# Three products of 12-bit parts for the plain own products of two layers of a graph network

## The chip, the cores and the metric

The kernel runs on one core of one Trainium2 chip. The metric is the device time of one execution in microseconds; the times shown are of three runs, and one further execution was profiled. In what follows PE is the matrix engine, PEld its weight loads, DVE the vector engine, ACT the scalar engine, POOL the general engine and SP the engine that only issues DMAs. Each engine works through its instructions in order.

## The reference

```python
def _edge_conv(x, src, dst, W, b):
    m = jnp.concatenate([x[dst], x[src] - x[dst]], axis=-1) @ W + b
    s = jax.ops.segment_sum(m, dst, num_segments=N)
    cnt = jax.ops.segment_sum(jnp.ones((dst.shape[0],), m.dtype), dst, num_segments=N)
    return s / jnp.maximum(cnt, 1.0)[:, None]

h = jnp.maximum(_layernorm(x, axis=-1), 0.0)
xs = [h]
for W, b in ((W0, b0), (W1, b1), (W2, b2)):
    h = jax.nn.relu(_edge_conv(h, src, dst, W, b))
    xs.append(h)
return x + jnp.concatenate(xs, axis=-1) @ Wf + bf
```

There are 2500 nodes of 256 features, 80000 edges sorted by destination, and three layers. With W split into its upper half Wt (for the destination) and its lower half Wb (for the difference), the sum over the edges of one destination is its degree times h(Wt - Wb), the "own" part, plus the product of a matrix of edge counts with z = h Wb.

## The kernel before

Nodes are padded to 20 tiles of 128 (NT); two tiles are a pair q, ten pairs. Features are kept turned, feature by node, in `hT` (two halves of 128 features, `hT[:, 0]` and `hT[:, 1]`), already multiplied by the degree, and `share` divides again where it is needed. The destinations are cut into five window groups, four of 504 columns and a last one, `alone`, of 486. `a_dram` holds the counts of edges, sources by destinations, one tensor to a group.

**Layer 0** builds the counts of one group while it multiplies those of the group before. `finish(g)` (line 904) stores a group's counts with four DMAs, from POOL's queue (from SP's for `alone`); for group 0 it also adds x to `acc` by accumulating DMAs (`add_x`, line 826). `acc`, 20 tiles of 256 columns in SBUF, collects the result. When group 4 begins, SP stores it to `acc_dram` (line 1136); layers 1 and 2 add their share there with accumulating DMAs on POOL's queue, and the bias bf is added there by four more (`add_bf`, line 1109), in layer 1's stream. In layer 0 the own products of groups 1 to 4 are already made of 12-bit parts: `split_own` (line 1083) makes three parts of hT (ACT rounds a high part, DVE subtracts to a low one, DVE combines both to a third), `forms_of_own` three of the weights, and three products in the fast float format replace one plain one.

**Layers 1 and 2** have two phases each. In the **node phase** (the loop over Q + LAG iterations, line 1431 on) each iteration multiplies one pair of node tiles by Wb and Wf with 12-bit parts (`Nodes.multiply`, from a `Split` of hT and `Forms` of the weights), ACT and DVE scale the result and split it into `zh` and `zl`, a high and a low part, sums for the later scheme go to `sh` and `sl`, and the pair of two iterations earlier (LAG = 2) is multiplied by the counts of `alone` (`Alone.multiply`). The lone group's own products are four plain ones, `own` (line 1350): two in early iterations, two in `end`. In the **stream phase** (`Stream.run`, line 1404) the other four groups go in two pairs by a scheme of seven products for a two by two block product. Chunk c of a pair (c = 0 to 4) has seven steps; a step multiplies one block by parts of z or of the sums, two tiles by a high and a low part each, so four products of 504 columns. That makes 70 steps, numbered 0 to 69, the second pair's from 35. The steps of a chunk are called b11, b21, b22, r1, r2, r3, r4. `Pair.make` (line 1260) makes their blocks out of a staged chunk: ACT casts five, DVE adds for r1 and r2 in place and makes r3 and r4 alone. Blocks are made LEAD = 5 steps ahead; there are seven buffers `block`. In chunk 4 each step has one more product, the own one, plain, of `ws` or the sums `wsum` of the weights with hT or sums of hT (`own_sum`, line 1276; `Pair.multiply`, line 1291). `take` (line 1308) then combines the seven results into hT. So there are 7 x 2 x 2 = 28 own products of pairs in the two layers.

The pool `stage` has four buffers of a chunk (1.0 MB from `a_dram`, two DMAs on SP). `Stream.make` asks for chunk m + 3 when chunk m is made. The node phase and the end of the stream use the same buffers for splits of hT. What is done besides, at a step n, stands in `tick` (line 1461): the combination of the weights, bf, the splits of the next layer's first node pairs, the next layer's forms, and, in layer 2, two loads of `acc_dram` back into `acc`.

**The end** multiplies the ten pairs of node tiles by the last part of Wf; DVE scales by `share` and adds `acc` (`add_to_acc`, line 1203), and the rows are stored.

Of the kernel before, what the change touches and what calls it, by code (L numbers as in the profile page):

```python
# [313 lines left out]
def by_windows(ctx: ExitStack, tc: tile.TileContext, x, src, dst, Ws, bs, Wf, bf, out, missing):  # L314
# [67 lines left out]
    acc = const.tile([P, NT, D], F32, name="acc")  # L382
# [3 lines left out]
    zl = const.tile([P, 2, Q * D + 32], F32R, name="zl")  # L386
    key_m = early.tile([P, NW + 1, CH, REP], BF16, name="key_m")
# [7 lines left out]
    ident_b = const.tile([P, P], BF16, name="ident_b")  # L395
    iota_m = const.tile([P, P], BF16, name="iota_m")
    iota_n = const.tile([P, NB], BF16, name="iota_n")
    deg = const.tile([P, WG, W + 1], F32, name="deg")
    gsum = const.tile([P, WG, W + 5], F32, name="gsum")
    nc_ = const.tile([P, W + 2], F32, name="nc_")  # L400
    deg_b = const.tile([P, WG, W + 1], BF16, name="deg_b")
    below = const.tile([P, CH, WG], F32, name="below")
    back_b = const.tile([P, P + 1], BF16, name="back_b")
# [59 lines left out]
    def load_wf(l, queue=SP):  # L463
        if l == L:
# [439 lines left out]
    def finish(g, a):  # L904
# [6 lines left out]
        if g == 0:  # L911
            for t in range(0, NT, 5):
                add_x(t, t + 5)
        yield
# [194 lines left out]
    def add_bf(k):  # L1109

        POOLo.dma_start(acc_dram[:, 5 * k:5 * k + 5, :],
                        bass.AP(tensor=bf.tensor, offset=bf.offset, ap=[[0, P], [0, 5], [1, D]]), accum_op=OP.add)

# [7 lines left out]
    for g in range(NG):  # L1121
        at = {}
        own = [NT] * 4 if g == 0 else [3, 3, 8, 8]
        if g + 1 < NG:
# [10 lines left out]
        else:  # L1135
            SPo.dma_start(acc_dram, acc)
# [35 lines left out]

    tmps = ctx.enter_context(tc.tile_pool(name="tmps", bufs=6))
    stage = ctx.enter_context(tc.tile_pool(name="stage", bufs=4))
    late = ctx.enter_context(tc.tile_pool(name="late", bufs=1))
    sh = late.tile([P, 2, Q * D + 32], F32R, name="sh")
    sl = late.tile([P, 2, Q * D + 32], F32R, name="sl")
    wsum = late.tile([P, 4, P], F32, name="wsum")

# [22 lines left out]

    def add_to_acc(t, po):
        DVEo.scalar_tensor_tensor(acc[:, t, :], po, share[:, t:t + 1], acc[:, t, :], op0=OP.mult, op1=OP.add)
# [41 lines left out]

    class Pair:

        def __init__(self, l, i):
            self.l, self.i = l, i  # L1250
            self.one, self.two = (slice(c0, c0 + n) for c0, n in map(group_of, pairs[i]))
            self.bank, self.r = {}, {}
# [23 lines left out]
        def own_sum(self, i):  # L1276
            one, two, r = self.one, self.two, self.r
            if i == 0:
                r["r1"] = tmp()[:, :GS]
                DVEo.tensor_add(r["r1"], hT[:, 0, one], hT[:, 0, two])  # L1280
            elif i == 1:
                r["r2"] = tmp()[:, :GS]
                DVEo.tensor_add(r["r2"], r["r1"], hT[:, 1, two])
            elif i == 2:
                r["r3"] = tmp()[:, :GS]
                DVEo.tensor_sub(r["r3"], hT[:, 0, one], r["r2"])
            elif i == 3:
                r["r4"] = tmp()[:, :GS]
                DVEo.tensor_add(r["r4"], r["r2"], hT[:, 1, one])

        def multiply(self, c, part, what, made):
# [3 lines left out]
            if c == Q // 2 - 1:  # L1295
                if part[0] == "x":
                    w = ws[self.l][0][:, part[2], part[1] * P:(part[1] + 1) * P]
                else:
                    w = wsum[:, part[1], :]
                m = {"b11": hT[:, 0, self.one], "b21": hT[:, 1, self.one], "b22": hT[:, 1, self.two]}.get(what)  # L1300
                PEo.matmul(to, w, self.r[what] if m is None else m, start=False, stop=False)
            for k, j in enumerate((2 * c, 2 * c + 1)):
                for z in range(2):
                    unit[0] = PEo.matmul(to, part_of(part, z, j), made[what][:, k, :],
                                         start=(c == 0 and k == 0 and z == 0),
                                         stop=(c == Q // 2 - 1 and k == 1 and z == 1))
# [27 lines left out]
    class Alone:  # L1334
# [15 lines left out]
        def own(self, o, c):  # L1350
            PEo.matmul(self.to[o], ws[self.l][0][:, c, o * P:(o + 1) * P],
                       hT[:, c, self.c0:self.c0 + self.n], start=(c == 0), stop=(c == DC - 1))

        def end(self):
            for o in range(DC):
                self.own(o, 1)
# [5 lines left out]
    def load_first(order):  # L1362
        c = order[0] // 2
        st = stage.tile([P, 4 * GS], F32R, name="staged").rearrange("p (t n) -> p t n", n=GS)
# [202 lines left out]
```

## Time and profile before

| | us |
|---|---|
| median of three runs | 462.43 |
| lowest, highest | 462.11, 462.63 |
| the profiled execution | 462.09 |
| its span, first to last instruction | 460.2 |
| node phase of layer 1 | 192.0 to 239.3 |
| stream of layer 1 | 239.3 to 315.4 |
| node phase of layer 2 | 315.4 to 364.2 |
| stream of layer 2 | 364.2 to 440.1 |
| the end's products | 440.1 to 455.7 |

The granted clock of PE was 1.000 over the whole span. Nearly all instructions have line 282 in the trace, that of the helper which keeps them in order, so they are told apart by tile names and shapes. A plain product of floats shows as two records, a product in the fast float format as one; both have the type f32 in the trace. Products are pipelined: one of 504 columns is shown as 0.39 us long, though the next may start before it ends. A row of a timeline may merge several instructions (x6); its duration is then from the first start to the last end.

### The profile page before, as it was taken

How to read it: one execution, taken by the hardware profiler on the slowest of the kernel's cores; microseconds unless marked ns; L12 is line 12 of the kernel's file. 1: busy time of each engine (PE TensorE's matmuls, PEld its weight loads, DVE VectorE, ACT ScalarE, POOL GpSimd, SP SyncE). 2: the span in 40 equal slices, each digit the busy share in tenths (PEclk: the TensorE clock that was granted, in tenths of full speed). 3: DMA queues.
4: the chain of work that ended last, by engine and by line, in shares of the span. 5: the costliest groups of instructions: out<-in, count | busy, mean ns of one | idle time of the engine just before them, and what ended most of it. 6: DMA issues, size and time to landing. Idle time of an engine off the chain costs nothing.

```text
span 460.2 us, 7512 instructions
## 1 busy us (share of the span) xinstructions
PE 452.0 (98%) x2729; PEld 356.6 (77%) x2729; DVE 353.2 (77%) x676; ACT 308.9 (67%) x595; POOL 62.6 (14%) x95
## 2 busy tenths in 40 slices
PE   8999999999999999999999999999999999999995
PEld 4888877677778778878878868867788787688685
DVE  7999979899888946178758758886877487569795
ACT  4878878694945434377769839756776897597540
POOL 4770006101001000022151000000212000000000
PEclk9999999999999999999999999999999999999999
DMA  8320088982908249685899999626578957520014
GB/s 277 101 58 13 1 171 130 204 174 42 184 1 168 60 171 432 230 231 118 208 333 183 193 186 208 110 90 184 66 154 215 354 184 291 204 92 0 1 64 164
DMA packets 30489, 71.90 MB, mean 156 GB/s; under 512 B 2427, under 2 KB 19150, under 8 KB 29550
## 3 DMA queue, kind: packets, MB, share of 16 engines
q1 hardware_dynamic: 17886, 47.71, 31.3%
q0 software_dynamic: 10784, 21.77, 28.7%
q10 hardware_dynamic: 1776, 1.89, 1.2%
q8 instruction: 22, 0.36, 0.3%
q14 instruction: 21, 0.17, 0.1%
HBM read 45.45 MB, written 28.69 MB: 161 GB/s over the span
## 4 chain that ended last, share of the span: by engine, by line
PE 94%; DVE 2%; DMA 2%; issue 0%; SPq 0%; DVEq 0%
PE bank L282 86%; PE pz L282 8%; DMA wbf<-in_L_gnn_Wf_dram 2%; PE turned L282 1%; DVE one_n L282 1%; DVE one_m L282 1%; DVE own_h L282 0%; DVE hT L282 0%; SPq L282 0%; DVE deg L282 0%; DVE acc L282 0%; DVE away L282 0%; DVE deg_b L282 0%; DVEq L282 0%
## 5 line engine op out<-in xcount | busy, mean ns | idle before, releaser
L282 ACT CAST block<-staged 128x1008 fp32r<-128x1008 bf16 x100 | 97.2, 1031 | 17.0 <-DVE staged L282 6.0
L282 PE MATMUL bank<-a,zh 128*128 128x504 f32 (+1 forms) x200 | 82.0, 410 | 0.0
L282 PE MATMUL bank<-a,zl 128*128 128x504 f32 (+1 forms) x200 | 77.9, 389 | 0.0
L282 PE MATMUL bank<-block,zh 128*128 128x504 f32 (+1 forms) x184 | 76.9, 418 | 0.0
L282 ACT CAST a<-bank 128x480 fp32r<-128x480 f32 (+1 forms) x105 | 54.3, 561 | 31.2 <-PE bank L282 30.9
L282 DVE TENSOR_TENSOR one_m<-iota_m,key_m 128x2048 bf16<-128x2048 bf16 (+2 forms) x55 | 64.1, 1165 | 9.4 <-PE bank L282 9.1
L282 PE MATMUL bank<-block,zl 128*128 128x504 f32 (+1 forms) x184 | 71.2, 387 | 0.0
L282 PE MATMUL bank<-block,sh 128*128 128x504 f32 x160 | 68.9, 431 | 0.0
L282 PE MATMUL bank<-block,staged 128*128 128x512 f32 (+1 forms) x288 | 62.8, 369 | 0.0
L282 PE MATMUL bank<-block,sl 128*128 128x504 f32 x160 | 62.6, 391 | 0.0
L282 PEld LDWEIGHTS bank<-block,staged 128*128 128x128 f32 x288 | 49.3, 188 | 10.2 <-issue 0.9
L282 DVE TENSOR_TENSOR block<-staged 128x1008 fp32r<-128x1008 bf16 x40 | 47.0, 1205 | 5.0 <-PE bank L282 3.5
L282 ACT ACTIVATE tmp<-bank,share 128x256 f32<-128x256 f32 x78 | 34.4, 471 | 23.8 <-PE bank L282 15.9
L282 POOL DMA_DIRECT2D acc_dram<-tmp x20 | 17.1, 853 | 191.9 <-ACT tmp L282 191.9
L282 PEld LDWEIGHTS bank<-a,zh 128*128 128x128 f32 x200 | 37.7, 188 | 6.6 <-ACT a L282 0.3
L282 PEld LDWEIGHTS bank<-a,zl 128*128 128x128 f32 x200 | 37.7, 189 | 6.2 <-issue 0.2
L282 DVE TENSOR_TENSOR one_n<-iota_n,key_n 128x640 bf16<-128x640 bf16 (+2 forms) x110 | 42.5, 428 | 0.0
L282 PEld LDWEIGHTS bank<-block,zh 128*128 128x128 f32 x184 | 34.6, 188 | 9.9 <-issue 2.3
L282 PEld LDWEIGHTS bank<-block,zl 128*128 128x128 f32 x184 | 34.6, 188 | 9.8 <-issue 3.2
L282 DVE TENSOR_TENSOR staged<-staged 128x1008 bf16<-128x1008 bf16 x40 | 27.2, 679 | 18.0 <-ACT block L282 15.8
L282 PEld LDWEIGHTS <-one_m 128*128 128x128 bf16 x834 | 30.3, 98 | 13.7 <-issue 7.0
L282 PE MATMUL pz<-wbf,hT 128*128 128x256 f32 x160 | 38.5, 385 | 0.2 <-DMA wbf<-in_L_gnn_Wf_dram 0.2
(195 smaller groups left out, 676.1 us busy)
## 6 DMA issues: line engine op xcount, KB each, us to landing
staged<-a_dram SPq DMA_DIRECT2D x40, 504.0 KB
a_dram<-a POOLq DMA_DIRECT2D x16, 630.0 KB, 7.8
block<-a_dram SPq DMA_DIRECT2D x16, 504.0 KB
acc_dram<-tmp POOLq DMA_DIRECT2D x20, 256.0 KB, 4.9
a_dram<-a SPq DMA_DIRECT2D x4, 1260.0 KB
acc_dram<-acc SPq DMA_DIRECT2D x1, 2560.0 KB
acc_dram<-in_L_gnn_bf_dram POOLq DMA_DIRECT2D x4, 640.0 KB, 33.2
acc<-acc_dram SPq DMA_DIRECT2D x2, 1280.0 KB
```

The source lines that it names most:

```text
L282: return self.tc.keep_in_program_order(call(*args, **kwargs))
```

## The change

- **Own products.** 23 of the 28 own products of the pairs, and the last two of the four of the lone group in each layer, become three products of 12-bit parts. In layer 1 r3 and r4 of the second pair stay plain, in layer 2 r2, r3 and r4. Each layer's weights are split once into `pair_w` (`PairForms`, on `ws` and on `wsum`), in the node phase. The split of the moving side is made by `own_high` (one ACT instruction) and `own_rest` (two DVE instructions) into one of three places in `spare`.
- **Where they stand.** The own product moves from chunk 4 to chunk 0 (b11, b21) or 2 (b22, r1) in the first pair, and to chunk 2 (b11, b21, b22) in the second (`OWN_AT`). `PLAN` lists, for each step, which job is done; steps -9 to -3 are iterations of the node phase. It takes the place of `tick`.
- **Buffers.** `stage` has three buffers; the splits of the first node pairs of the next layer use the places in part. The lone group's first blocks are loaded into `spare` in layer 1 and into two blocks in layer 2. The chunk loads are asked for from iteration 8 on.
- **Bias and acc.** The bias is added to `acc` in SBUF by four accumulating DMAs behind the stores of group 2 in layer 0; `acc` is stored to `acc_dram` when group 3 begins. Its memory is then free. At the end its copy is loaded from `acc_dram` into `zl` and `zh` by six DMAs (`back`, step 63 of layer 2), DVE adds from there and writes to a `tmp` that is stored.

```diff
-    acc = const.tile([P, NT, D], F32, name="acc")
+    acc = early.tile([P, NT, D], F32, name="acc")
...
         if g == 0:
             for t in range(0, NT, 5):
                 add_x(t, t + 5)
+        if g == 2:
+            for t in range(0, NT, 5):
+                POOLo.dma_start(acc[:, t:t + 5, :],
+                                bass.AP(tensor=bf.tensor, offset=bf.offset, ap=[[0, P], [0, 5], [1, D]]), accum_op=OP.add)
...
+        if g + 2 == NG:
+            SPo.dma_start(acc_dram, acc)
...
-    stage = ctx.enter_context(tc.tile_pool(name="stage", bufs=4))
+    stage = ctx.enter_context(tc.tile_pool(name="stage", bufs=3))
...
+    spare = late.tile([P, 9 * 512], F32R, name="spare")
+    pair_w = late.tile([P, 3, 2, 4 * P], F32R, name="pair_w")
+    places = [[spare[:, (3 * i + k) * 512:(3 * i + k + 1) * 512] for k in range(3)] for i in range(3)]
...
+    class PairForms:
+        def high(self):
+            ACTo.activation(self.parts[0], self.raw, AF.Copy, scale=C1 * DOWN)
+        def low(self):
+            DVEo.scalar_tensor_tensor(self.rest, self.raw, C1, self.parts[0].bitcast(F32), op0=OP.mult, op1=OP.subtract)
+        def across(self):
+            ACTo.activation(self.parts[1], self.rest, AF.Copy, scale=E12)
+        def less(self):
+            DVEo.scalar_tensor_tensor(self.rest, self.parts[0].bitcast(F32), -1.0 / E12, self.rest, op0=OP.mult, op1=OP.add)
+        def last(self):
+            ACTo.activation(self.parts[2], self.rest, AF.Copy, scale=1.0 / C1)
+
+    OWN_AT = [{"b11": 0, "b21": 0, "b22": 2, "r1": 2}, {"b11": 2, "b21": 2, "b22": 2}]
...
+        def own_high(self, what, place):
+            h = self.own_of(what)
+            self.own[what] = [p[:, :GS] for p in places[place]]
+            ACTo.activation(self.own[what][0], self.r[what] if h is None else h, AF.Copy, scale=DOWN)
+
+        def own_rest(self, what):
+            h = self.own_of(what)
+            high, low, across = self.own[what]
+            DVEo.tensor_sub(low, self.r[what] if h is None else h, high.bitcast(F32))
+            DVEo.scalar_tensor_tensor(across, low.bitcast(F32), -E12, high.bitcast(F32), op0=OP.mult, op1=OP.add)
...
-            if c == Q // 2 - 1:
+            own_at = OWN_AT[self.i].get(what, last)
+            if c == own_at:
+                if what in self.own:
+                    w = (1, part[1]) if part[0] == "s" else (0, 2 * part[2] + part[1])
+                    for k, p in enumerate(self.own.pop(what)):
+                        PEo.matmul(to, pair_w[:, k, w[0], w[1] * P:(w[1] + 1) * P], p, start=(c == 0 and k == 0), stop=False)
...
         def end(self):
             for o in range(DC):
-                self.own(o, 1)
+                for k in range(3):
+                    PEo.matmul(self.to[o], pair_w[:, k, 0, (2 + o) * P:(3 + o) * P], self.parts[k], start=False, stop=(k == 2))
...
+    PLAN = [{
+        -9: "form.0.high combine", -8: "form.0.low form.1.high", -7: "form.0.across form.1.low", -6: "form.0.less form.1.across alone_high.2",
+        -5: "form.0.last form.1.less alone_rest high.0.b11.0", -4: "form.1.last rest.0.b11 high.0.b21.1", -3: "rest.0.b21",
+        5: "high.0.b22.2 sum.0.r1", 7: "rest.0.b22", 8: "high.0.r1.0", 10: "rest.0.r1", 11: "sum.0.r2",
+        13: "high.0.r2.1", 15: "rest.0.r2", 17: "sum.0.r3", 19: "high.0.r3.2", 21: "rest.0.r3", 22: "sum.0.r4", 24: "high.0.r4.0", 26: "rest.0.r4",
+        36: "high.1.b11.1", 38: "rest.1.b11", 39: "high.1.b21.0", 41: "rest.1.b21", 42: "high.1.b22.2", 44: "rest.1.b22", 45: "less",
+        46: "sum.1.r1", 48: "sum.1.r2", 50: "high.1.r1.1", 51: "sum.1.r3", 52: "rest.1.r1 sum.1.r4", 53: "high.1.r2.2 node.0.0", 54: "rest.1.r2",
+        55: "node_rest.0", 57: "node.1.-", 59: "node_rest.1", 60: "node.2.-", 62: "node_rest.2", 64: "next", 65: "next_low", 66: "next_across", 67: "next_last",
+    }]
+    PLAN.append({**PLAN[0], 45: "", 53: "node.0.0", 54: "", 63: "back", 65: "next_low node.3.-", 68: "node_rest.3", 69: "begin"})
...
+        def back():
+            for z, a, b in ((zl, 16, NT), (zh, 0, 8), (zh, 8, 16)):
+                q = a % 16 // 2
+                for i in range(2):
+                    SPo.dma_start(z[:, i, q * D:(q + (b - a) // 2) * D].bitcast(F32).rearrange("p (q d) -> p q d", d=D),
+                                  acc_dram[:, a + i:b:2, :])
...
+            if i >= Q - 2:
+                stream.load((1, 1, 2, 3)[i - Q + 2])
...
-            add_to_acc(t, po[k])
+            DVEo.scalar_tensor_tensor(sums[:, k, :], po[k], share[:, t:t + 1], acc_of(t), op0=OP.mult, op1=OP.add)
```

More of the change, by code (lines that the diff above doesn't have):

```diff
@@ L1360, in by_windows, with load_first @@
     loaded = {}
[L1362 to L1365 removed]
+    def load_first():
+        st = spare[:, :4 * GS].rearrange("p (t n) -> p t n", n=GS)
+        SPo.dma_start(st.bitcast(F32), a_dram[alone][:, 0:4, :])
         for p in range(2):
[L1367 to L1368 removed]
+            loaded[p] = st[:, 2 * p:2 * p + 2, :]
     def load_alone(p, order):
@@ L1426, in by_windows, with next_forms, jobs @@
         if l == 1:
-            load_first(order)
-            split(order[2])
+            load_first()
+            split(order[2]).rest()
         pending = []
         stream = Stream(l)
+        after = orders[l + 1]
+        two = stream.steps[0][1], stream.steps[-1][1]
+        new_raw(l + 1)
+        forms = PairForms(l, 0, ws[l][0].rearrange("p c n -> p (c n)")), PairForms(l, 1, wsum.rearrange("p s n -> p (s n)"))
+        nodes = {}
+        def next_forms():
+            raw = flat(l + 1)
+            coming[:] = [Forms(raw, [raw[:, c, :] if l + 1 < L else raws[L][:, c, 0, :] for c in range(DC)])]
+            coming[0].high()
+        def back():
[4 more added lines that the diff above has]
+                                  acc_dram[:, a + i:b:2, :])
+        jobs_of = {
+            "sum": lambda i, r: two[i].own_sum(r), "high": lambda i, w, k: two[i].own_high(w, k), "rest": lambda i, w: two[i].own_rest(w),
+            "alone_high": lone.high, "alone_rest": lone.rest,
+            "combine": lambda: combine(wsum, ws[l][0].rearrange("p c (o n) -> p (c o) n", o=2)),
+            "form": lambda i, step: getattr(forms[i], step)(),
+            "node": lambda k, place: nodes.update({k: split(after[k], place)}), "node_rest": lambda k: nodes[k].rest(),
+            "less": lambda: DVEo.tensor_sub(ws[l + 1][0], ws[l + 1][0], ws[l + 1][1]),
+            "next": next_forms, "next_low": lambda: coming[0].low(), "next_across": lambda: coming[0].across(),
+            "next_last": lambda: coming[0].last(), "begin": lambda: begun.append(split_in_blocks(6, False)), "back": back,
+        }
+        def jobs(n):
+            for job in PLAN[l + 1 == L].get(n, "").split():
+                name, *args = job.split(".")
+                jobs_of[name](*(int(a) if a.isdigit() else None if a == "-" else a for a in args))
         for i in range(Q + LAG):
@@ L1440, in by_windows @@
                 if i + AHEAD_H < Q and order[i + AHEAD_H] not in splits:
[L1441 removed]
+                    split(order[i + AHEAD_H]).rest()
                 pending.append(n)
```

132 lines of the change are left out of this document (56 added, 76 removed).

## The prediction

> **What bounds the kernel now.** I read the page's busy shares and the chain that ended last, then the busy time by stage.
>
> ```profile
> PE 452.0 (98%) x2729; PEld 356.6 (77%) x2729; DVE 353.2 (77%) x676; ACT 308.9 (67%) x595; POOL 62.6 (14%) x95
> PE 94%; DVE 2%; DMA 2%; issue 0%; SPq 0%; DVEq 0%
> 239.30:315.40 76.10, 76.10 (x310) 57.80 (x309) 57.88 (x76) 55.99 (x64) 2.70 (x2) 1.00 0.83 167
> 364.20:440.10 75.90, 75.90 (x310) 57.62 (x309) 57.02 (x77) 55.05 (x64) 0.00 (x0) 1.00 0.38 134
> ```
>
> The first line is the page's, the second the chain's; the other two are stretches (length, then busy time of PE, weight load, DVE, ACT and POOL, granted clock, DMA share, GB/s): the pair streams of layers 1 and 2, 70 steps each. PE is busy throughout at clock 1.00, and 94% of the chain is PE. A busy PE need not be at its peak, so what a product costs is read from the distance of starts. In the streams DVE is busy 57.88 of 76.10 us and ACT 55.99: these two have room, and the question is how much of it the change uses up.
>
> **The change part by part.**
>
> *The products.* The timeline of PE gives the prices.
>
> ```profile
> 245.80 0.39 PE L282 MATMUL bank<-block,zh 128*128 128x504 f32 x1
> 252.19 0.39 PE L282 MATMUL bank<-block,zh 128*128 128x504 f32 x1
> 302.94 1.00 PE L282 MATMUL bank<-hT,wt 128*128 128x504 f32 x2
> 313.50 1.01 PE L282 MATMUL bank<-tmp,wt 128*128 128x504 f32 x2
> 275.60 1.01 PE L282 MATMUL bank<-tmp,wt 128*128 128x504 f32 x2
> 237.70 1.79 PE L282 MATMUL bank<-hT,wt 128*128 128x486 f32 x4
> 239.56 0.39 PE L282 MATMUL bank<-block,zl 128*128 128x504 f32 x1
> 137.36 0.85 PE L282 MATMUL bank<-own_h,own_w 128*128 128x504 f32 x3
> 172.92 1.48 PE L282 MATMUL bank<-own_h,own_w 128*128 128x486 f32 x6
> L282 PEld LDWEIGHTS bank<-own_h,own_w 128*128 128x128 f32 x48 | 8.6, 189 | 1.3
> ```
>
> From 245.80 to 252.19 lie seven steps of four products: 6.39/28 = 0.228 us each, 0.913 a step. From 302.94 to 313.50 lie six steps that have a plain own product as well: 10.56/6 = 1.760 a step, so a plain own product (two records) costs 0.847. The three products that replace it are already in the trace, in layer 0: three of 504 columns end 0.85 after the first starts, which is two distances of 0.23 and the 0.39 of the last. Three cost 0.685, and each replacement saves 0.162 us. Twelve of the pairs' products change in layer 1 (all but r3 and r4 of the second pair) and eleven in layer 2 (r2 too stays plain): 23 x 0.162 = 3.73 us. Of the lone group's own products the two of the second half change in each layer. Today's two take 239.56 - 0.228 - 237.70 = 1.63 us, one 0.816 (a product of the stream stands between them and 239.56). Six in 1.48 us are five distances of 0.22 and one length of 0.38, so three cost 0.66: 4 x 0.156 = 0.62. **PE loses 4.35 us.** The added weight loads (three for two) stay under the products, as layer 0's 0.19 do under 0.22.
>
> The Trainium skill, FP8 and Floating Point Precision, TensorE Precision Notes, says that a true FP32 product makes four passes through the array. Four of the stream's products would be 0.913 us; the trace has 0.847, so the rule is nearly right and the rows decide; by it the change would save 27 x 0.228 = 6.2 us.
>
> *The splits.* Each takes one ACT and two DVE instructions.
>
> ```profile
> L282 ACT ACTIVATE own_h<-hT 128x504 fp32r<-128x504 f32 x6 | 3.8, 636 | 4.8 <-PE bank L282 2.2 <-DVE hT L282 2.1 <-ACT a L282 0.5
> 240.00 5.69 ACT L282 CAST block<-staged 128x1008 fp32r<-128x1008 bf16 x6
> 274.62 0.67 DVE L282 TENSOR_TENSOR hT<-bank,tmp 128x504 f32<-128x504 f32 x1
> 275.21 0.67 DVE L282 TENSOR_TENSOR staged<-staged 128x1008 bf16<-128x1008 bf16 x1
> 278.30 2.31 DVE L282 TENSOR_TENSOR block<-staged 128x1008 fp32r<-128x1008 bf16 x2
> 309.12 0.69 DVE L282 TENSOR_TENSOR staged<-hT,staged 128x512 fp32r<-128x512 f32 x1
> 309.84 0.69 DVE L282 SCALAR_TENSOR_TENSOR staged<-staged 128x512 fp32r<-128x512 f32 x1
> 244.08 0.42 DVE L282 TENSOR_TENSOR wsum<-wt 128x256 f32<-128x256 f32 x1
> 244.53 0.62 DVE L282 TENSOR_TENSOR wsum<-wsum,wt 128x128 f32<-128x128 f32 x2
> 214.50:219.00 4.50, 4.50 (x22) 3.68 (x21) 3.46 (x8) 3.27 (x8) 0.84 (x1) 1.00 0.75 177
> 228.00:232.50 4.50, 4.50 (x22) 3.70 (x21) 2.48 (x6) 2.34 (x5) 0.85 (x1) 1.00 1.06 341
> ```
>
> A split costs ACT 0.64. DVE's instructions start 0.60 apart where they are independent (274.62 and 275.21), the two large ones that make blocks 1.12 each, and one that needs the result before it comes 0.72 later (309.12 and 309.84): a split is 0.72 + 0.60 = 1.32.
>
> Layer 1's stream gets ten splits: DVE 57.88 + 13.2 - 1.0 (the combination of the weights, 0.42 and 0.62, goes into the node phase) = 70.1 us, ACT 55.99 + 6.4 = 62.4 us. PE will need 76.10 - 12 x 0.162 = 74.2. Both fit in total, DVE narrowly. The tightest place is the second pair of layer 1, from step 41 to step 62. Between the last block made for each, DVE has three chunks of blocks (each 2 x 0.60 + 2 x 1.12 = 3.44), six splits, four own sums and the difference of the next weights: 10.3 + 7.9 + 2.4 + 0.6 = 21.2 us. PE takes 21 x 0.913 + 3 x 0.685 = 21.2 us for these steps. So there DVE works as long as PE, and what keeps PE from waiting is the lead it starts with: the two blocks of 278.30 are done at 280.61, step 35 began at 277.4 (275.60 and one plain step) and step 41 begins 6 x 0.913 later, at 282.9, 2.3 us after its block is there. That lead stays unless DVE itself waits. If the cover goes, PE is late by what DVE waited beyond 2.3 us. In layer 2 one split and the difference are missing, 1.9 us more room.
>
> In the node phase an iteration is 4.5 us of PE, with DVE busy 3.46 and ACT 3.27 (2.48 and 2.34 in the last two, which split no nodes). Over seven iterations DVE gets 1.0 + 4 x 0.6 + 3 x 1.32 = 7.4 us of 5 x 1.04 + 2 x 2.02 = 9.2, ACT nine instructions of 0.64, 5.8 of 10.5. The fullest iteration (a weight step and the lone group's split) overruns by 0.9 us; the zl that is then late is read two iterations later. I take nothing for this; without that cover 0.9 us a layer.
>
> I put 0.35 us for small stalls (from nothing to 4 us), near the nothing that the balance gives.
>
> *Staging in three buffers.* A chunk's load now waits until the chunk three before it is made into blocks.
>
> ```profile
> 245.80:252.20 6.40, 6.40 (x30) 5.26 (x29) 5.01 (x6) 6.34 (x7) 0.00 (x0) 1.00 0.98 196
> 383.40:389.80 6.40, 6.40 (x30) 5.26 (x29) 3.61 (x5) 4.92 (x6) 0.00 (x0) 1.00 0.88 321
> ```
>
> From then to its first use are 14 steps less the 5 of lead, 8.2 us. A chunk is 1.0 MB: 5.3 us at the 196 GB/s of layer 1, 3.2 at the 321 of layer 2. It fits, and layer 1 also loses the bias traffic. I take nothing; if it took 9.2 us, PE would wait up to 1 us in each of seven chunks.
>
> *The bias and acc.* Four accumulating DMAs leave POOL's queue in layer 1's stream and stand in layer 0 behind the stores of window group 2; the store of acc is moved one group earlier on SP, behind the bias and ahead of the next layer's weights.
>
> ```profile
> acc_dram<-in_L_gnn_bf_dram POOLq DMA_DIRECT2D x4, 640.0 KB, 33.2
> acc<-in_x_dram POOLq DMA_DIRECT2D x3, 640.0 KB, 14.3
> L282 POOL DMA_DIRECT2D acc_dram<-in_L_gnn_bf_dram x4 | 6.3, 2222 | 2.0 <-DMA acc_dram<-tmp 2.0
> 111.80 1.58 POOL L282 DMA_DIRECT2D a_dram<-a  x3 [23.43 <-ACT a L282]
> 116.25 0.53 POOL L282 DMA_DIRECT2D a_dram<-a  x1 [2.88 <-ACT a L282]
> 139.37 1.58 POOL L282 DMA_DIRECT2D a_dram<-a  x3 [22.59 <-ACT a L282]
> 163.89 0.39 SPq L282 DMA_DIRECT2D one_m<-in_L_gnn_W_dram  x1
> 174.56 1.04 ACT L282 ACTIVATE block<-one_m 128x1024 fp32r<-128x1024 f32 x1
> ```
>
> The bias is issued from 116.8 on, at most 2.2 us each, to 125.7, and lands 14.3 us later (the same kind of DMA into acc) or 33.2 (today's bias): at 140 or 159. The next stores on that queue come at 139.4 and are read in layer 1. The 2.5 MB of acc then take some 8 us at 321 GB/s, to 148 or 167; the weights, issued at 163.9 today, are read at 174.6. Hidden by either bound; PE would be late only past that, by what is over.
>
> At the end the six loads of acc's copy into zl and zh wait for PE's last reads: the last of them for step 62, seven steps, one split product and three plain ones, 9.6 us, before the stream's end.
>
> ```profile
> 441.71 0.88 DVE L282 SCALAR_TENSOR_TENSOR acc<-bank,share,acc 128x256 f32<-128x256 f32 x2 [0.74 <-PE bank L282]
> 455.17 0.48 DVE L282 SCALAR_TENSOR_TENSOR acc<-bank,share,acc 128x256 f32<-128x256 f32 x1 [0.17 <-PE bank L282]
> ```
>
> The first use is at 441.7, of the two tiles loaded first; the last 1 MB, about 3.2 us, belongs to the last pairs of tiles. Nothing. The end after PE (455.2 to 460.2) is untouched.
>
> **Sum.** The profiled execution took 462.09 us, its span 460.2 and 1.9 around it; it becomes 462.09 - 4.35 + 0.35 = 458.1. The median shown is 462.43, 0.34 above, so the forecast is **458.4**.
>
> **The rivals.**
>
> *A, DVE becomes the bound (slower).* DVE's own waits in the two streams speak for it.
>
> ```profile
> DVE staged L282 <- ACT block L282: 7.1, 5, 3.2
> DVE staged L282 <- ACT block L282: 8.7, 5, 2.8
> ```
>
> The first is layer 1's, the second layer 2's: total, times, longest. The sum that makes r2 overwrites what ACT must have copied first. If these waits stay in full, DVE needs 70.1 + 7.1 = 77.2 us for 76.1 today, and in layer 2 57.02 + 9 x 1.32 - 1.0 + 8.7 = 76.6 for 75.9: 1.8 us more, less the lone group's 0.6, **463.6**. It is slower once more than 6 us a stream remain. Against it: DVE waits there because it is ahead of PE (ACT is held by blocks that PE has not released), and a late DVE finds them copied. The Trainium skill, VectorE: DVE Perf Modes, The DRAIN you can't avoid, has the next instruction wait until the pipe empties, full lengths with no overlap; the 0.60 us between starts of 0.67 us disagrees. By full lengths the 21.2 us would be 22.9, and 0.6 of the lead would be left. Chance 0.08.
>
> *B, a wait takes part of the gain.* DVE late at step 62, or a chunk's load behind its buffer: one to three us back, **460.4** in the middle. For it: the equal budgets and three buffers. Against: lead and load times above. 0.13.
>
> *C, the gain is given back.* As B with 4 us back, or the plain products' cost is a bubble after them that the order around keeps: **462.4**. Against: layer 0 shows three products without one. 0.07.
>
> *D, four passes.* The plain product costs 0.913, hidden from the distances by lost records: 462.43 - 6.2 = **456.3**. The six equal steps speak against it. 0.04.
>
> **How the numbers follow.** The forecast has 0.68, between 457.5 and 459.4 (stalls from nothing to 1.3 us, and 0.5 of scatter below). With D and B, faster by over 0.2% (0.9 us, about what a measurement of this kernel can tell from no change) has 0.85; C is the middle, 0.07; A is 0.08. The range reaches from 457.3 through most of B to 461.0, which leaves out D, C and A and little of B.
>
> **What would show it.** Steps with a split own product should be 1.60 us, from start to start, for 1.76; the streams 74.2 and 74.1 us; PE's weight loads should have no wait for DVE's blocks at steps 56 to 62 of layer 1. Wrong would be: distances over 0.23 between the three parts, PE waiting for `block`, `spare` or `staged`, the weights of layer 1 landing after 174, or PE in the last stage waiting for zl or zh.

## The result, and the profile after

| | before | after |
|---|---|---|
| median, us | 462.27 | 458.19 |
| lowest to highest (4 runs each) | 462.11 to 462.63 | 457.85 to 458.58 |
| ratio to before, 95% interval | | 0.9911 (0.9894 to 0.9928) |
| profiled execution, its span | 462.09, 460.2 | 457.85, 456.0 |

The kernel is 4.08 us faster in the medians, 4.24 in the two profiled executions; the forecast for the profiled one was 458.1, for the median 458.4.

The page of the changed kernel, busy shares (busy time, share of the span, instructions) and the chain that ended last:

```profile
PE 447.2 (98%) x2756; PEld 362.0 (79%) x2756; DVE 387.5 (85%) x734; ACT 326.0 (71%) x632; POOL 63.0 (14%) x95
PE 95%; DVE 2%; DMA 2%; issue 0%; SPq 0%; DVEq 0%
```

PE lost 4.8 us of busy time and DVE gained 34.3, yet PE is still the chain. The windows of the two streams of the changed kernel (length, then busy time of PE, weight load, DVE, ACT, POOL, then granted clock, DMA share, GB/s):

```profile
239.00:312.90 73.90, 73.90 (x321) 60.10 (x320) 67.29 (x91) 60.98 (x74) 0.00 (x0) 1.00 0.39 123
361.50:435.60 74.10, 74.10 (x320) 59.93 (x319) 66.74 (x93) 59.71 (x74) 0.00 (x0) 1.00 0.43 139
```

Each stream is about 2 us shorter, and DVE fills 67.3 of 73.9 us where it filled 57.9 of 76.1. In layer 1 the DMA share fell from 0.83 to 0.39; the bias is no longer added there, and in the kernel before with three buffers and the bias moved it is 0.42.

PE's timeline of the changed kernel gives the price of a split product, and the place where the stream begins:

```profile
237.69 2.17 PE L282 MATMUL bank<-spare,pair_w 128*128 128x486 f32 x9
239.69 0.40 PE L282 MATMUL bank<-block,zh 128*128 128x504 f32 x1
239.92 0.39 PE L282 MATMUL bank<-block,zl 128*128 128x504 f32 x1
...
271.02 0.84 PE L282 MATMUL bank<-spare,pair_w 128*128 128x504 f32 x3
...
272.62 0.85 PE L282 MATMUL bank<-spare,pair_w 128*128 128x504 f32 x3
```

From 271.02 to 272.62 lies one step with its own product in three parts: 1.60 us, as forecast. The first row holds the lone group's six parts and the first own product of the stream, so that here the stream itself begins 3 x 0.23 us ahead of 239.69, at 239.01.

The table of stages, for all kernels of this study, is from PE's timeline of each. A node phase begins with its first product of 512 columns, a stream 0.23 us (one distance) ahead of its second product of 504 columns from a block, the end with its first product of 256 columns; "rest" reaches from there to the end of the span. The first own product, where it stands in parts ahead of the first block, so counts in the node phase (0.69 us). The ratio is to runs of the kernel before beside each kernel.

| kernel | median, us | ratio to before | start | node 1 | stream 1 | node 2 | stream 2 | rest |
|---|---|---|---|---|---|---|---|---|
| before | 462.27 | 1 | 190.60 | 48.73 | 75.96 | 48.83 | 75.97 | 20.11 |
| after | 458.19 | 0.9911 | 190.58 | 49.11 | 73.26 | 49.26 | 73.42 | 20.37 |
| plain products, splits made | 462.18 | 0.9997 | 190.51 | 49.58 | 75.00 | 49.71 | 75.02 | 20.18 |
| bias back in layer 1 | 463.72 | 1.003 | 190.62 | 49.10 | 77.87 | 49.26 | 73.42 | 20.33 |
| before, three buffers | 467.17 | 1.0116 | 190.88 | 48.73 | 80.55 | 48.84 | 75.94 | 20.06 |
| before, three buffers, bias early | 462.34 | 1.0001 | 190.76 | 48.73 | 75.94 | 48.85 | 75.95 | 20.17 |
| second pairs split twice | 470.94 | 1.0191 | 190.56 | 49.11 | 80.14 | 49.26 | 76.30 | 22.13 |
| first pairs split twice | 469.72 | 1.0165 | 190.63 | 50.05 | 78.53 | 49.26 | 77.85 | 21.38 |
| lone group all in parts | 459.02 | 0.9924 | 190.61 | 50.53 | 73.26 | 49.66 | 73.42 | 20.42 |
| all 28 of the pairs | 463.29 | 1.002 | 190.78 | 49.10 | 72.93 | 51.31 | 72.93 | 24.45 |
| own sums on POOL | 464.03 | 1.004 | 190.79 | 49.10 | 76.52 | 49.26 | 75.91 | 21.12 |
| all 28, own sums on POOL | 468.32 | 1.0135 | 190.86 | 49.10 | 76.17 | 50.99 | 75.37 | 24.01 |
| acc stored twice | 463.36 | 1.0034 | 192.22 | 54.53 | 73.26 | 49.26 | 73.42 | 20.51 |
| acc stored behind the weights | 458.34 | 0.992 | 190.63 | 49.11 | 73.26 | 49.26 | 73.42 | 20.82 |

The stages are of the profiled execution, which is not always near the median: it took 462.36 us with the bias back and 469.38 with the second pairs split twice, the shortest of theirs, and 459.83 with the lone group all in parts and 465.03 with acc stored twice, the longest of theirs. One execution of the kernel with the own sums on POOL, 552.9 us at a granted clock of 0.753, is in the slow state and left out of its median.

With those 0.69 us put back where they belong, the change took 0.31 and 0.26 us from the node phases (forecast 0.31 each), 2.01 and 1.86 from the streams (forecast 12 x 0.162 = 1.94 and 11 x 0.162 = 1.78): 4.44 us for a forecast of 4.35. The rest grew by 0.26.

### The profile page after: what moved, and what is told of

The parts are those of the page before. It is cut to its first block, busy times and chain, and to the rows that moved or that the text cites. A ratio compares the mean times of both kernels' runs of the same rounds, so it can differ in the third digit from the quotient of the medians.

```text
span 456.0 us, 7686 instructions
## 1 busy us (share of the span) xinstructions
PE 447.2 (98%) x2756; PEld 362.0 (79%) x2756; DVE 387.5 (85%) x734; ACT 326.0 (71%) x632; POOL 63.0 (14%) x95
## 3 DMA queue, kind: packets, MB, share of 16 engines
q10 hardware_dynamic: 1776, 1.89, 1.2%
## 4 chain that ended last, share of the span: by engine, by line
PE 95%; DVE 2%; DMA 2%; issue 0%; SPq 0%; DVEq 0%
PE bank L282 86%; PE pz L282 8%; DMA wbf<-in_L_gnn_Wf_dram 2%; PE turned L282 1%; DVE one_m L282 1%; DVE one_n L282 1%; DVE hT L282 0%; SPq L282 0%; DVE own_h L282 0%; DVE deg L282 0%; DVE tmp L282 0%; DVE away L282 0%; DVE deg_b L282 0%; DVEq L282 0%
## 5 line engine op out<-in xcount | busy, mean ns | idle before, releaser
L282 PE MATMUL bank<-block,zh 128*128 128x504 f32 (+1 forms) x192 | 75.6, 394 | 0.0
L282 PE MATMUL bank<-block,zl 128*128 128x504 f32 (+1 forms) x192 | 74.2, 387 | 0.0
L282 PE MATMUL bank<-block,sh 128*128 128x504 f32 x160 | 63.7, 398 | 0.0
L282 PE MATMUL bank<-block,staged 128*128 128x512 f32 (+1 forms) x264 | 58.6, 372 | 0.0
L282 PEld LDWEIGHTS bank<-block,staged 128*128 128x128 f32 x264 | 45.6, 188 | 9.6 <-issue 0.9
L282 PEld LDWEIGHTS bank<-block,zh 128*128 128x128 f32 x192 | 36.1, 188 | 8.0 <-DVE staged L282 0.2
L282 PEld LDWEIGHTS bank<-block,zl 128*128 128x128 f32 x192 | 36.0, 188 | 7.9 <-issue 0.5
L282 PE MATMUL bank<-one_n,one_m 128*128 128x60 bf16 x834 | 36.2, 195 | 0.2 <-DVE one_n L282 0.2
```

Of the source, the lines that this page charges most:

```text
L282: return self.tc.keep_in_program_order(call(*args, **kwargs))
```

## The experiments

**Are the plain products the gain?** All splits are made, and the products read the plain operands again.

```diff
-                    for k, p in enumerate(self.own.pop(what)):
-                        PEo.matmul(to, pair_w[:, k, w[0], w[1] * P:(w[1] + 1) * P], p, start=(c == 0 and k == 0), stop=False)
+                    self.own.pop(what)
+                    m = self.own_of(what)
+                    plain = wsum[:, part[1], :] if w[0] else ws[self.l][0][:, part[2], part[1] * P:(part[1] + 1) * P]
+                    PEo.matmul(to, plain, self.r[what] if m is None else m, start=(c == 0), stop=False)
...
-                for k in range(3):
-                    PEo.matmul(self.to[o], pair_w[:, k, 0, (2 + o) * P:(3 + o) * P], self.parts[k], start=False, stop=(k == 2))
+                PEo.matmul(self.to[o], ws[self.l][0][:, 1, o * P:(o + 1) * P], hT[:, 1, self.c0:self.c0 + self.n],
+                           start=False, stop=True)
```

> All splits are still made and all products stand where the change puts them, but the 23 own products of the pairs and the 4 of the lone group are plain again. Theory: 23 x 0.162 + 4 x 0.156 = 4.35 us come back, 462.5, streams of 75.9 us (layer 1: 12 x 0.162 = 1.94 more, layer 2: 11 x 0.162 = 1.78 more). Rival (part of the gain is the new places of the products, the buffers or the DMAs): 461.5 or less.

462.18 us, ratio 0.9997 (0.9988 to 1.0006): the whole gain is gone, at the places where products were exchanged. Against the changed kernel the node phases are 0.47 and 0.45 us longer (two lone products and the first own one: 2 x 0.156 + 0.162 = 0.47), the streams 1.74 and 1.60 (11 x 0.162 = 1.78 and 10 x 0.162 = 1.62). Two starts of its own products in PE's timeline are 1.76 us apart:

```profile
271.87 1.01 PE L282 MATMUL bank<-tmp,wsum 128*128 128x504 f32 x2
...
273.63 1.01 PE L282 MATMUL bank<-tmp,wsum 128*128 128x504 f32 x2
```

So the gain is the price of the products, and the splits, the new plan and the three buffers together cost nothing that shows.

**What is the bias's new place for?** The bias goes back to layer 1's stream.

```diff
-        if g == 2:
-            for t in range(0, NT, 5):
-                POOLo.dma_start(acc[:, t:t + 5, :],
-                                bass.AP(tensor=bf.tensor, offset=bf.offset, ap=[[0, P], [0, 5], [1, D]]), accum_op=OP.add)
...
         def jobs(n):
+            if l == 1 and n in (6, 13, 20, 27):
+                k = n // 7
+                POOLo.dma_start(acc_dram[:, 5 * k:5 * k + 5, :],
+                                bass.AP(tensor=bf.tensor, offset=bf.offset, ap=[[0, P], [0, 5], [1, D]]), accum_op=OP.add)
```

> The bias goes back into layer 1's stream (four accumulating DMAs on POOL's queue at steps 6, 13, 20 and 27), all else as in the changed kernel. Theory (the gain is the price of the products alone): same as the changed kernel, 458.2 within 0.4 us, streams 73.9 and 74.1 us; the weights of layer 1 land by about 176 again instead of 181. Rival (the relief of the DMA queues in layer 1's stream gave part of the gain): 459.2 or more, layer 1's stream longer than 74.5.

463.72 us, ratio 1.003 (1.0018 to 1.0043), in the rival's range. In the profiled execution all of the loss is in stream 1, 4.61 us longer than after. Waits of this kernel in layer 1's stream (total, times, longest), and one stretch of it:

```profile
ACT block L282 <- DMA staged<-a_dram: 7.6, 4, 6.0
DVE staged L282 <- DMA staged<-a_dram: 7.0, 2, 6.2
...
PEld bank L282 <- ACT block L282: 5.0, 8, 1.5
```

```profile
245.80:252.20 6.40, 6.40 (x30) 5.26 (x29) 6.23 (x9) 5.45 (x7) 0.00 (x0) 1.00 0.87 64
```

The same stretch of the changed kernel:

```profile
245.80:252.20 6.40, 6.40 (x30) 5.26 (x29) 6.23 (x9) 5.42 (x7) 0.00 (x0) 1.00 0.55 180
```

With the bias the DMA engines are busy 0.87 of the time and move 64 GB/s; without it they are busy 0.55 and move 180. Whose bytes these are shows by queue (packets, MB, share of 16 engines; q0 carries the accumulating DMAs, q1 the loads of chunks), from 244 to 255 us, first with the bias back, then in the kernel before:

```profile
q0 software_dynamic: 657, 0.66, 76.9%
```

```profile
q1 hardware_dynamic: 489, 1.52, 53.2%
q0 software_dynamic: 485, 0.48, 45.5%
```

With the bias back, the loads that SP issues from 244.52 on move nothing in these 11 us, where 8.2 are allowed for a chunk: all bytes are the bias's. In the kernel before, with the same bias traffic, the loads move 1.52 MB beside it, and no such waits arise. Why the loads get half of the engines in one kernel and nothing in the other, no trace here shows. Is it the buffers, then? The next two runs ask that of the old kernel.

**Three buffers in the kernel before, with the bias in its stream and without.** The fourth buffer keeps its size but holds only one split. The second kernel also has the bias and the store of acc where the changed kernel has them.

```diff
-    stage = ctx.enter_context(tc.tile_pool(name="stage", bufs=4))
+    stage = ctx.enter_context(tc.tile_pool(name="stage", bufs=3))
+    first = ctx.enter_context(tc.tile_pool(name="first", bufs=1))
...
-                split(after[(n - 49) // 7])
+                split(after[(n - 49) // 7], first if n == 49 else None)
```

> The kernel before (plain products, bias in layer 1's stream) with three staging buffers for the chunks; the fourth keeps its size and holds only the split of the next layer's first node pair. Theory (three buffers and the bias's traffic together make the chunks late, as the run with the bias put back showed, 4.61 us in layer 1's stream): layer 1's stream +4 to +5 us, with ACT's and DVE's block makers waiting for staged<-a_dram; layer 2's stream 0; 466.3 to 467.3. Rival (what was lost there came from the new order of jobs or of the queues, not from the buffers): 462.3 +- 0.5. Second rival (three buffers cost by themselves, bias or not): both streams longer, 467 or more.

> As the one above, and the bias is added in layer 0 and acc stored one group earlier, as in the changed kernel; products still plain. Theory: without the bias's traffic three buffers fit, both streams as before (75.9 us each), and the weights of layer 1 are late without PE being late: 462.3, from 461.8 to 462.9. Rival (three buffers cost by themselves): both streams longer by 1 us or more, 464 or above. Second rival (the new place of the bias in layer 0 costs time): start of layer 1 later than 191.0, 462.9 or above.

467.17 us, ratio 1.0116 (1.0098 to 1.0135), with stream 1 4.59 us longer and every other stage within 0.3 us of before; and 462.34, ratio 1.0001 (0.9991 to 1.001), with every stage within 0.2 us of before. The first kernel's waits and stretch in layer 1:

```profile
ACT block L282 <- DMA staged<-a_dram: 11.4, 3, 7.4
DVE staged L282 <- DMA staged<-a_dram: 10.5, 2, 7.8
PEld bank L282 <- ACT block L282: 6.6, 11, 2.6
```

```profile
245.80:252.20 6.40, 6.40 (x29) 5.27 (x28) 4.96 (x7) 6.25 (x8) 0.00 (x0) 1.00 0.75 63
```

Four buffers with the bias: 75.96 us in stream 1. Three with the bias: 80.55. Three without: 75.94. Neither is dear alone; the two together cost 4.6 us. So the move of the bias earns nothing, but pays for the buffer that makes room for the splits.

**How much DVE time is left in the streams?** The second half of each split of the second pair, or of the first, is made twice.

```diff
-            "rest": lambda i, w: two[i].own_rest(w),
+            "rest": lambda i, w: [two[i].own_rest(w) for _ in range(2 if i == 1 else 1)],
```

> DVE's part of each split of the second pair is done twice: 5 x 1.32 us more DVE in layer 1, 4 x 1.32 in layer 2. Theory (the cover is DVE's lead, 0.7 us at step 62 of layer 1 and 2.4 in layer 2, and what it waits itself before that, about 1 us): PE late by 5 to 6 us in layer 1 and 1.7 to 2.9 in layer 2, 465 to 467. Rival (only the total counts, and a stream has 73.9 - 67.3 = 6.6 us of DVE to spare): within 1 us of the changed kernel.

> The same for the first pairs, seven splits, of which b11 and b21 lie in the node phase. Theory: the lead there is 2.3 us at step 13 and 2.5 at step 27, and about 1.5 us of DVE's own waits can go; four doublings before step 27 are 5.3 us, so PE is late by 1.2 to 2.8 us a layer, 460.6 to 463.8, less than for the second pairs. Rival (only the total counts): within 1 us of the changed kernel, and equal to the run with the second pairs.

Second pairs: 470.94 us, ratio 1.0191 (1.0176 to 1.0207); stream 1 is 6.88 us longer, stream 2 2.88, the rest 1.76. First pairs: 469.72, ratio 1.0165 (1.015 to 1.0181); node 1 0.94, stream 1 5.27, stream 2 4.43, the rest 1.01. Both cost more than either theory said. PEld's waits at the second pair of layer 1, with the second pairs doubled:

```profile
PEld bank L282 <- ACT block L282: 4.6, 2, 2.7
PEld bank L282 <- DVE block L282: 1.5, 2, 1.1
```

PE's weight loads wait for ACT's blocks three times as long as for DVE's. The first pair shows why. DVE's and ACT's timelines of the kernel with the first pairs doubled, and then DVE's of the changed kernel:

```profile
256.46 1.47 DVE L282 TENSOR_TENSOR staged<-staged 128x1008 bf16<-128x1008 bf16 x2
```

```profile
257.25 1.97 ACT L282 CAST block<-staged 128x1008 fp32r<-128x1008 bf16 x2 [4.24 <-DVE staged L282]
```

```profile
251.81 1.46 DVE L282 TENSOR_TENSOR staged<-staged 128x1008 bf16<-128x1008 bf16 x2
```

DVE's two sums for r1 and r2 start 4.65 us later (256.46 for 251.81), and ACT, which casts what they made, stands idle 4.24 us for them, with all later casts behind. So the longer waits come by the sum that ACT must still cast, which the prediction had not watched; the block that DVE makes alone, which it had, is waited for as well, but less.

**Can DVE be relieved?** POOL, idle in the streams, makes the own sums.

```diff
-                DVEo.tensor_add(r["r1"], hT[:, 0, one], hT[:, 0, two])
+                POOLo.tensor_add(r["r1"], hT[:, 0, one], hT[:, 0, two])
...
-                DVEo.tensor_add(r["r4"], r["r2"], hT[:, 1, one])
+                POOLo.tensor_add(r["r4"], r["r2"], hT[:, 1, one])
```

> The changed kernel with the eight own sums of each layer's stream (r1 to r4 of both pairs, 0.60 us of DVE each) on POOL, which stands idle there. Theory (DVE's lead, short as it is, is never used up, so relief gives nothing; POOL's nearest row is 0.60 us for 256 columns with one input, 1.2 us for 504 columns, at most 2.4 with two inputs, and a sum has two steps, 1.8 us, before ACT reads it): 458.2, from 457.7 to 459.5, streams 73.9 and 74.1 or up to 1.3 longer in all. Rival (DVE's lateness costs something hidden in the changed kernel): under 457.7. Second rival (POOL's sums are late for ACT's high part, or slow DVE down): 460 or above, with ACT's own splits and casts waiting for POOL.

464.03 us, ratio 1.004 (1.0026 to 1.0054): the second rival, with stream 1 3.26 us longer and stream 2 2.49. Of its two reasons only one holds: no engine waits for POOL in either stream, so its sums are not late, but DVE is slowed. POOL's and DVE's timelines of this kernel, in two places:

```profile
238.71 1.62 POOL L282 TENSOR_TENSOR tmp<-tmp,hT 128x504 f32<-128x504 f32 x1
240.41 1.58 POOL L282 TENSOR_TENSOR tmp<-hT,tmp 128x504 f32<-128x504 f32 x1
...
278.20 1.72 POOL L282 TENSOR_TENSOR tmp<-tmp,hT 128x504 f32<-128x504 f32 x1
```

```profile
239.12 1.76 DVE L282 TENSOR_TENSOR spare<-hT,spare 128x504 fp32r<-128x504 f32 x1
240.91 1.63 DVE L282 SCALAR_TENSOR_TENSOR spare<-spare 128x504 fp32r<-128x504 f32 x1
...
278.71 0.67 DVE L282 TENSOR_TENSOR tmp<-bank,tmp 128x504 f32<-128x504 f32 x1
```

Instructions of DVE that take 0.68 us alone take 1.63 and 1.76 beside a sum of POOL, while the one that reads `bank`, in PSUM, beside the POOL sum of 278.20 takes 0.67. A sum that is moved saves DVE 0.60 us, and holds it up by about 1 us where it meets such an instruction. POOL makes the first pair's four sums at the change from the node phase to the stream, and DVE's first two blocks of the stream come 4.03 us later than in the changed kernel (here first):

```profile
245.68 2.33 DVE L282 TENSOR_TENSOR block<-staged 128x1008 fp32r<-128x1008 bf16 x2
```

```profile
241.65 2.33 DVE L282 TENSOR_TENSOR block<-staged 128x1008 fp32r<-128x1008 bf16 x2
```

Sums on POOL at places where DVE reads PSUM were not tried. The Trainium skill, SBUF — State Buffer, Who interferes with whom, says that a DVE instruction with two inputs in SBUF and a GpSimd instruction that reads SBUF exclude each other, and that one with at most one SBUF input, outside the two-port modes, does not contend. These rows agree with both halves.

**Can more products be exchanged?** First the lone group's other two products (their own split, products in iteration 8), then all 28 of the pairs, then these with the sums on POOL. Of the plan's long lines the cuts show only the parts that change.

```diff
-    -8: "form.0.low form.1.high", -7: "form.0.across form.1.low",
+    -8: "form.0.low form.1.high alone_high.1.0", -7: "form.0.across form.1.low alone_rest.0",
...
-    -4: "form.1.last rest.0.b11 high.0.b21.1", -3: "rest.0.b21",
+    -4: "form.1.last rest.0.b11", -3: "high.0.b21.1", -2: "rest.0.b21",
...
-            if 0 < i <= DC:
-                lone.own(i - 1, 0)
+            if i == 8:
+                lone.own(0)
```

> The other two own products of the lone group in each layer are made of three parts too (split at iterations 4 and 5 of the node phase, products at iteration 8; b21's split of the first pair one iteration later). Theory: 4 x 0.156 = 0.62 us less, 457.6, each node phase 0.31 us shorter (48.1 and 48.3 for 48.4 and 48.6), since DVE has room there. Rival (DVE's fullest iterations, which overrun, take it back): 458.2 or more, node phases no shorter.

```diff
-    60: "node.2.-", 62: "node_rest.2", 64: "next",
+    60: "node.2.- high.1.r3.3", 62: "node_rest.2", 63: "rest.1.r3 high.1.r4.4", 64: "rest.1.r4 next",
...
-    45: "", 53: "node.0.0", 54: "", 63: "back",
+    45: "", 63: "rest.1.r3 high.1.r4.4 back",
```

> The five plain own products left in the pairs are made of parts too, their splits in places of sh and sl that are free by then. Theory: PE has 5 x 0.162 = 0.81 us less, but the splits stand ahead of the next forms on DVE, 2.7 us in layer 1, where the forms are ready only 0.3 to 1 us before the next node phase: PE late there by about 2 to 2.5 us, in layer 2 by up to 0.5; 459 to 460.5. Rival (DVE's load is no limit): 457.4.

> All 28 own products of the pairs in parts, as in the run of that name (463.29), with the own sums on POOL. Theory (that run lost 2.05 us in layer 2's node phase and 2.3 in the end because DVE was late with the next forms and splits): 2.4 us less DVE work in each second pair takes back most of it, 458 to 460.5; if all of it, 457.4, better than the changed kernel. Rival (the loss came from ACT's three to four added instructions or from the order in which these stand, not from DVE's load): 462.5 to 463.8. Second rival (POOL's sums late): above 464.

The lone group in parts: 459.02 us, ratio 0.9924 (0.991 to 0.9937), 0.8 above the changed kernel in the medians. Instead of 0.31 us less, node 1 takes 1.42 more and node 2 0.40 more in the profiled execution, the longest of five; the shortest took 458.18, so the loss varies. All 28: 463.29, ratio 1.002 (1.0011 to 1.0029). The streams give 0.33 and 0.49 us as priced (2 x 0.162 and 3 x 0.162), but node 2 loses 2.05 and the rest 4.08. ACT's timeline at the change of layers, and PE's in the end, of that kernel:

```profile
312.33 1.18 ACT L282 ACTIVATE block<-wbf 128x512 fp32r<-128x512 f32 x2 [4.26 <-DVE wbf L282]
```

```profile
446.24 0.38 PE L282 MATMUL bank<-block 128*128 128x256 f32 x1 [0.86 <-DVE block L282]
446.96 1.46 PE L282 MATMUL bank<-block 128*128 128x256 f32 x10 [0.34 <-DVE block L282]
```

The added DVE instructions of steps 63 and 64 stand ahead of the next forms and of the end's splits, and come out in the stage behind. In the rest, PE's products take 2.31 us longer (437.05 to 454.44, in the changed kernel 435.63 to 450.71), and DVE's last sum ends 1.40 us behind them, where it ended 0.51 behind. With the sums on POOL it is 468.32, ratio 1.0135 (1.0118 to 1.0152): node 2 and the rest hardly better (50.99 and 24.01), the streams 3.24 and 2.44 us worse. Relief that blocks DVE is none, so that run cannot tell DVE's load from ACT's; the rows above, in which ACT and PE wait for DVE, speak for DVE's, without showing it.

**How near was the late bias?** First a second store of acc ahead of layer 1's weights, into a buffer that nothing reads; then the one store behind the weights.

```diff
         if g + 2 == NG:
             SPo.dma_start(acc_dram, acc)
+            SPo.dma_start(dram.tile([P, NT, D], F32, name="acc_more"), acc)
```

> SP stores acc a second time, to a tensor nobody reads, ahead of the weights of layer 1. Theory (the weights stand behind the store in SP's queue and landed at 181; the splits made from them were ready at 188.9, 1.7 us before PE's first use of the weights at 190.6): the weights land about 8 us later and PE is late by about 6 us, 464. Rival (stores and loads of one queue share the engines, so that the weights are late by less than the store takes): PE late by 0 to 3 us, 458.2 to 461.

```diff
-        if g + 2 == NG:
-            SPo.dma_start(acc_dram, acc)
...
                     raw_of_next()
+                    SPo.dma_start(acc_dram, acc)
```

> The changed kernel with the store of acc issued on SP behind the two loads of layer 1's weights in place of ahead of them. Theory (in the changed kernel these weights land 6 us later than before, at 180.5 in place of 174.6, and that costs nothing, since what is made of them is ready by 188.9 and first used at 190.6): weights read at 174 to 176 again, and the time stays, 458.2, from 457.6 to 458.8. Rival (their lateness costs the first iterations of layer 1 something, since DVE and ACT make the forms and the splits late): 457.5 or less. Second rival (acc's store, now later, holds up what takes its memory in layer 1): 459 or above, with a wait for it after 182.

463.36 us, ratio 1.0034 (1.0019 to 1.005): in the profiled execution layer 1 starts 1.64 us later and its node phase is 5.42 longer. And 458.34, ratio 0.992 (0.9906 to 0.9933): the changed kernel's time. ACT's first use of the weights in the two, the doubled store first:

```profile
187.19 1.06 ACT L282 ACTIVATE block<-one_m 128x1024 fp32r<-128x1024 f32 x1 [12.59 <-DMA one_m<-in_L_gnn_Wf_dram]
```

```profile
174.97 1.06 ACT L282 ACTIVATE block<-one_m 128x1024 fp32r<-128x1024 f32 x1 [0.28 <-DMA one_m<-in_L_gnn_Wf_dram]
```

At 187.19 the weights cost 7 us in the profiled execution and 5.2 in the medians, at 181.11 (after) and 174.97 nothing. The last version takes the lateness away without a gain in time; nothing in the study was faster than the changed kernel.

## Why the prediction was right, and where not

**The products: right, by their own rows.** 1.60 us a step was forecast and measured; 4.35 us in all was forecast, 4.44 measured, and the run with plain products gave each stage its share back within 0.04. The time came 0.25 us below the forecast of 458.1: about 0.1 more from the products and 0.35 not lost in stalls, less 0.26 in the rest. Rival D, four passes (0.228 us more for each of 27 products than for three), is out by the same rows: its 6.2 us would show as steps of 1.83 us where the plain ones have 1.76.

**The allowance of 0.35 us for stalls: not needed.** PEld's waits and DVE's waits for ACT in the streams, layer 1 first:

```profile
PEld bank L282 <- issue: 0.9, 4, 0.2
DVE staged L282 <- ACT block L282: 2.5, 3, 1.3
...
DVE staged L282 <- ACT block L282: 2.8, 3, 1.6
PEld bank L282 <- issue: 0.9, 4, 0.2
```

In layer 1 PE's weight loads wait for no block at all, in layer 2 for 0.2 us twice. DVE's waits for ACT fell from 7.1 and 8.7 us to 2.5 and 2.8: rival A needed more than 6 a stream, and they went as the prediction argued, a late DVE finding its blocks copied. Its forecast of 70.1 us for DVE in layer 1 was 2.8 too high (67.29); some 2 us of that are no saving, since three instructions of `take` start only behind the stream's end, at 313.49, 314.20 and 314.80.

**"That lead stays unless DVE itself waits": too hopeful.** DVE's timeline in layer 1, with the blocks that it makes for steps 41 and 62 and the one wait between, and PE's first products of these steps, in the changed kernel:

```profile
277.09 2.32 DVE L282 TENSOR_TENSOR block<-staged 128x1008 fp32r<-128x1008 bf16 x2
...
282.28 0.68 DVE L282 TENSOR_TENSOR staged<-staged 128x1008 bf16<-128x1008 bf16 x1 [0.79 <-ACT block L282]
...
299.62 2.32 DVE L282 TENSOR_TENSOR block<-staged 128x1008 fp32r<-128x1008 bf16 x2
```

```profile
281.30 0.39 PE L282 MATMUL bank<-block,zh 128*128 128x504 f32 x1
...
302.57 0.39 PE L282 MATMUL bank<-block,zh 128*128 128x504 f32 x1
```

At step 41 (281.30) the blocks are 1.89 us old, at step 62 (302.57) only 0.63, where 2.3 was forecast for both. PE took the 21.2 us of the working (21.27), DVE 22.53: 0.79 of the 1.3 more is the one wait for ACT, the exception that the prediction named and did not price, and the rest is in starts that lie up to 0.18 further apart than the sum had them. And the doubled splits show PE waiting longer for ACT's casts behind DVE's sums than for these blocks, a chain that the working had not followed. The forecast held because the need stayed just below the cover, not because the cover was 2.3 us; that 0.63 was enough is luck. The 0.6 us of lead that the prediction got from full lengths came out nearly to the number, but not by them: independent starts lie 0.60 apart here too (295.13, 295.72, 296.32). The Trainium skill, VectorE: DVE Perf Modes, The DRAIN you can't avoid, also says that a next instruction that is not held starts earlier, which the prediction left out; with that, the 0.60 us is no disagreement.

**The node phase: room in sum, none in place.** 7.4 of 9.2 us was forecast to fit and did: the two phases gave what was priced. But with one split more, and the products and one other split moved for it, layer 1's took 1.42 us longer in the profiled execution. A sum over seven iterations does not show the room at one place.

**Staging in three buffers: "it fits" was right for a reason given half.** The working put the loss of the bias traffic beside the three buffers as a bonus. It is the condition: with the bias back, no byte of a chunk's load moved from 244 to 255. The 196 GB/s that stood for the load's speed were not the load's alone either: the bias's bytes are in it.

**The bias and acc: the mis-sized term.** The bias was to land at 140 or 159, acc to be stored by 167, and the weights to be read at 174.6. Timelines of the changed kernel on POOL, SP, ACT and DVE, and the wait of SP:

```profile
116.75 6.11 POOL L282 DMA_DIRECT2D acc<-in_L_gnn_bf_dram  x4
```

```profile
161.50 0.36 SPq L282 DMA_DIRECT2D acc_dram<-acc  x1
163.87 0.37 SPq L282 DMA_DIRECT2D one_m<-in_L_gnn_W_dram  x1
```

```profile
SPq L282 <- DMA acc<-in_L_gnn_bf_dram: 146.3, 3, 130.4
```

```profile
181.11 1.06 ACT L282 ACTIVATE block<-one_m 128x1024 fp32r<-128x1024 f32 x1 [6.47 <-DMA one_m<-in_L_gnn_Wf_dram]
```

```profile
188.24 0.69 DVE L282 SCALAR_TENSOR_TENSOR block<-block 128x512 fp32r<-128x512 f32 x1
```

The bias landed at 161.5, outside both bounds: the row of the same kind, x into acc, was taken for its landing, but four of these stand behind each other and behind a_dram's stores in POOL's queue. The weights came at 181.1, which the prediction had listed as a sign of being wrong. It cost nothing, because the step's second half was wrong as well: what PE needs is not the weights at 174.6, but the forms made of them and, last on DVE, the splits behind these, ready at 188.93, and PE's first product with them starts at 190.58. "Late only past that, by what is over" would have given 6.5 us; there were still at least 1.65 us of slack. The doubled store, 6.1 us later, went over it and lost 7.1 in start and node phase, more than what was over; 2.5 us of PE's waits there are for the lone group's first block, whose load came late too:

```profile
PE bank L282 <- DMA spare<-a_dram: 2.5, 1, 2.5
```

**The end: right.** Its copies of acc are not waited for. The rest is 0.26 us longer; its scatter between kernels with the same code there (20.18 to 20.82) is as large.

## What to carry to other kernels

Price a replaced instruction by the distance of starts in a steady stretch, and multiply: that was good to 2%. A sum of busy times says whether an engine can keep up, not whether it can do so at each place; follow the first consumer that is itself an engine with a queue (here ACT's cast behind DVE's sum), and look for slack in that chain. An idle engine is no free help where its work holds up the one that it relieves. Where a change takes a buffer away and moves traffic elsewhere in one go, price them together, since each may be free and the pair not.

## What the runs showed of the hardware

- Accumulating DMAs that add one broadcast row are slow for the bytes they move: alone, from 244 to 255 us with the bias back, they take 76.9% of the DMA engines' time for 0.66 MB, where the changed kernel's loads of chunks take 57.4% for 2.04 MB; in layer 0 four of 640 KB took until 44.7 us after the first issue (116.75 to 161.50).
- POOL's sum of 504 columns takes 1.3 to 1.8 us, and a DVE instruction with both inputs in SBUF waits for it in full (0.68 becomes 1.63 to 1.76); one with an input in PSUM does not.
- In the profiled execution of the changed kernel the granted clock was 1.00 as long as PE had products, which end at 450.71, and 0.53 from 452.5 on, where PE has nothing to do; before, it stayed at 1.00 to the end. So the drop costs nothing, and the end's products take as long as before (15.08 us, before 15.04):

```profile
436.00:451.00 15.00, 14.71 (x111) 14.08 (x109) 13.87 (x30) 4.40 (x6) 0.00 (x0) 1.00 0.42 139
452.50:456.00 3.50, 0.00 (x0) 0.00 (x0) 0.00 (x0) 0.00 (x0) 0.00 (x0) 0.53 0.07 22
```
